# Middle group's rows dealt in turn, and four of 24 C products on GpSimd with their sums two units later

## Chip, cores and metric

The kernel runs on one core of a Trainium2 chip. The metric is the device time in microseconds of one execution. The kernel before takes 13000.71 us (median of 3 runs, 12998.91 to 13001.96).

## What is computed

Two metaformer layers over an input of 2 x 96 x 128 x 128 (float32). Layer 0 mixes tokens with four selective scans (Mamba): along the rows, along the rows backwards, along the columns and along the columns backwards. Layer 1 mixes them with a 3x3 convolution. Each mixer and each feed-forward network follows a layer norm and is added to its input. Nearly all of the time is in the scans:

```python
xz = x @ in_w.T;  xc, z = split(xz)              # 192 + 192 channels per direction
xc = silu(causal_conv4(xc) + conv_b)
dt_raw, Bm, Cm = split(xc @ xproj_w.T)           # 6, 16 and 16 values per token
dt = softplus(dt_raw @ dt_w.T + dt_b)
h = exp(dt * A) * h + dt * B_t * u_t             # per channel, 16 states, 16384 tokens in turn
y = sum over the 16 states of h * C_t
out = ((y + Dp * xc) * silu(z)) @ outp_w.T       # then the four directions are fused by fuse_w
```

## The kernel before

**Steps, groups, units.** Per image (two of them) the scan stage runs over two pairs of directions, (0, 2) and (1, 3), each in 32 tiles of T = 512 tokens: 64 steps per image, 128 in all. The two directions of a pair have 2 x 192 = 384 channels, which are 3 groups of 128 partitions. Group 1, the middle one, holds the last 64 channels of the first direction in partitions 0 to 63 and the first 64 of the second in partitions 64 to 127. A unit is one group and two of the 16 states, (g, s) in the code, so a step has 24 units: 0 to 7 are group 0, 8 to 15 group 1, 16 to 23 group 2.

**What a unit does.** GpSimd multiplies a row tile of B by dt*u (`b_part`, L324). ScalarE makes two decays exp(dt*A) into PSUM (`decay`, L330). VectorE runs two scans of 512 tokens (`scan`, L334), which overwrite the decays in PSUM, and one product with C over both states (L409), which overwrites the C rows in SBUF. ScalarE copies the last state to `hst` (L410). TensorE adds the two products to y in PSUM with an identity matrix (`sums`, L341). At a group's first unit y starts with Dp*xc (L416), after `gated` (L349) has taken the previous group's y; y has one PSUM buffer.

**Rows.** B and C are needed on all 128 partitions. `rows_out` (L255) copies the 96 rows of one step to SBUF and writes four copies to DRAM (`bcd`, L261). `row_tile` (L312) reads them back, broadcast over the partitions: 128 x 4 states x 512, 1 MB, for two units. A group 1 tile comes in two DMAs of 64 partitions. B has four such buffers, C has three (`bufs=ahead + 1`).

**The order is written by hand.** `in_order` keeps every engine in program order, SP's queue of DMA issues too; a DMA that must wait for its buffer holds all that stands behind it on SP. Iteration k of the main loop issues: on even k the fetch of B for units k+6 and k+7; GpSimd's product with B for unit k+2; the pieces listed for (k, 0); the first scan of unit k; `behind(k-1)`, which is the product with C, the state copy and the sums of unit k-1; the second scan; on even k the fetch of C for units k+4 and k+5; the decays of unit k+2; the pieces listed for (k, 1). `later` puts a piece into a later iteration.

**The next step's preparation** is spread over the 24 units by the list `at` (L301): loads at 0, the convolution of groups 0 to 2 on TensorE at 4, 5, 6 (`conv`, copied out by ScalarE in `conv_out`, L233), the gates at 7, 10, 11 (`gate`, `gate_out`, L241), silu of all of xc at (8, 1) and of sz at (14, 1) (L244, with an activation table load before and after), the rows at 12, and dt in three chains from 13, 18 and 21. All of these, `project` (L352, in iterations 3 and 19) included, use the one PSUM bank `misc`, so each waits until ScalarE has emptied the bank of the one before.

Of the kernel before, what the change touches and what calls it, by code (L numbers as in the profile page):

```python
# [10 lines left out]
F32 = mybir.dt.float32  # L11
# [3 lines left out]
AF = mybir.ActivationFunctionType  # L15
# [5 lines left out]
C = 96  # L21
W = 128
L = W * W
T = 512
# [4 lines left out]
DI = 192  # L29
HID = 384  # L30
PAIRS = ((0, 2), (1, 3))
NG = 3
# [1 line left out]
B_AHEAD = 3  # L34
C_AHEAD = 2
AHEAD = 2
BY_POOL = ()
BCO = 32
NBC = 4 * S

# [2 lines left out]
def tile_metaformer(ctx: ExitStack, tc: tile.TileContext, a: dict, out: bass.AP):  # L43
    nc = tc.nc
# [22 lines left out]
    convb = const("convb", (128, 2, NG))  # L67
    bcw = const("bcw", (128, 2, NG, BCO + NBC))
    dtw = const("dtw", (2 * RK, 2, NG * 128))
# [6 lines left out]
    dmat = cpool.tile([128, 2, NG, 128], F32, name="dmat")  # L76
    gmat = cpool.tile([128, 2, NG + 1, C], F32, name="gmat")
    inx = cpool.tile([C, 4, 4, DI], F32, name="inx")
    nc.vector.memset(gmat, 0.0)
    with tc.tile_pool(name="prep", bufs=1) as pp, tc.tile_pool(name="prep_ps", bufs=2, space=PSUM) as pps:  # L80
        alog = pp.tile([128, 2, NG, S], F32, name="alog")
        nc.sync.dma_start(alog, a["alog"])
        nc.scalar.activation(alog, alog, AF.Exp)
        nc.vector.tensor_scalar_mul(amat, alog, -1.0)

        dskip = pp.tile([128, 2, NG], F32, name="dskip")
        nc.sync.dma_start(dskip, a["dskip"])
        for pi in range(2):
            for g in range(NG):
                nc.vector.tensor_scalar_mul(dmat[:, pi, g, :], ident, dskip[:, pi, g : g + 1])  # L90

        inxw = pp.tile([C, 4, DI], F32, name="inxw")
        nc.sync.dma_start(inxw, a["inx"])
        taps = pp.tile([C, 4, 4, DI], F32, name="taps")
        nc.sync.dma_start(taps, a["taps"].broadcast_to((C, 4, 4, DI)))
        for d in range(4):
            nc.vector.tensor_tensor(inx[:, d], taps[:, d], inxw[:, d, None, :].broadcast_to((C, 4, DI)), ALU.mult)
        outw = pp.tile([C, 4, DI], F32, name="outw")
        nc.sync.dma_start(outw, a["outw"])
        fusew = pp.tile([C, 4, C], F32, name="fusew")  # L100
        nc.sync.dma_start(fusew, a["fusew"])
        for pi, (da, db) in enumerate(PAIRS):

            pieces = [
                (slice(0, 128), da, 0, 128),
                (slice(0, 64), da, 128, 192),
                (slice(64, 128), db, 0, 64),
                (slice(0, 128), db, 64, 192),
            ]
            for g, (rows, d, lo, hi) in enumerate(pieces):  # L110
                ps = pps.tile([128, C], F32, name="ps")
                nc.tensor.matmul(ps[rows, :], outw[:, d, lo:hi], fusew[:, d, :], start=True, stop=True)
                nc.vector.tensor_copy(gmat[rows, pi, g, :], ps[rows, :])

    def layernorm(x, eps, dst, wp, psp, bufs=2, **cast):

# [66 lines left out]
    def mamba(acc, xnr, xnc):  # L183

        with ExitStack() as st:
# [24 lines left out]
            def prologue(pi, i, d):  # L210
# [19 lines left out]
                def conv_out(g):  # L230
                    if g == 0:
                        d["xc"] = two.tile([128, NG, T], F32, name="xc")
                    nc.scalar.activation(d["xc"][:, g, :], d["ps"], AF.Identity, bias=convb[:, pi, g : g + 1])  # L233

                def gate(g):
                    d["ps"] = inproj(pi, g, lambda dd, k, lo, hi: inz[:, dd, lo:hi], src, (3,))
# [1 line left out]
                def gate_out(g):  # L238
                    if g == 0:
                        d["sz"] = two.tile([128, NG, T], F32, name="sz")  # L240
                    nc.scalar.copy(d["sz"][:, g, :], d["ps"])  # L241

                def silu(name):
                    nc.scalar.activation(d[name], d[name], AF.Silu)  # L244
# [8 lines left out]
                        )  # L253

                def rows_out():  # L255

                    d["rows"] = one.tile([BCO + NBC, T], F32, name="rows")
                    nc.scalar.copy(d["rows"], d["ps"][0 : BCO + NBC, :])
                    d["bcd"] = rows_d.tile([COPIES, 2, NBC // 2, T], F32, name="bcd")
                    for n in range(COPIES):  # L260
                        nc.sync.dma_start(d["bcd"][n].rearrange("k r t -> (k r) t"), d["rows"][BCO:, :])  # L261
# [37 lines left out]


                at = [(0, 0, load), (8, 1, partial(silu, "xc")), (14, 1, partial(silu, "sz"))]  # L301
                at += [(12, 0, rows), (12, 1, rows_out)]
                for g, k in enumerate((4, 5, 6)):
                    at += [(k, 0, partial(conv, g)), (k, 1, partial(conv_out, g))]
                for g, k in enumerate((7, 10, 11)):
# [6 lines left out]
            def row_tile(d, g, s, k, ahead):  # L312

                t = gen.tile([128, 4, T], F32, name=f"row{k}", bufs=ahead + 1)
                for half in range(2) if g == 1 else (slice(None),):
                    rows = slice(half * 64, half * 64 + 64) if g == 1 else half
                    at = s + S * (half if g == 1 else g // 2)
                    n = (64 if g == 1 else 128) // COPIES
                    src = d["bcd"][None, :, k, at : at + 4, :].broadcast_to((n, COPIES, 4, T))
                    nc.sync.dma_start(t[rows], src)  # L320
                return t
# [17 lines left out]
            def sums(s, y, c):  # L339
                for j in range(2):  # L340
                    nc.tensor.matmul(y, ident, c[:, j, :], start=False, stop=s + j == S - 1)  # L341

            def by_pool(s, y, h, c):
                nc.gpsimd.tensor_tensor(c, h, c, ALU.mult)
                sums(s, y, c)

            def gated(pi, d, g, y):
                t = d["sz"][:, g, :]
# [26 lines left out]
            def later(k, where, f, *args):  # L375
                todo.setdefault((k, where), []).append(partial(f, *args))
# [26 lines left out]
            def behind(k):  # L403

                n, u = divmod(k, nu)
                (pi, i), d, (g, s) = steps[n], state[n], units[u]
                h, c = hs.pop(k), cs.pop(k)
                if (g, s) not in BY_POOL:
                    nc.vector.tensor_tensor(c, h, c, ALU.mult)  # L409
                nc.scalar.copy(hst[:, g, s : s + 2], h[:, :, T - 1])  # L410
                if s == 0:
                    if k > 0:
                        pn, pu = divmod(k - 1, nu)
                        gated(steps[pn][0], state[pn], units[pu][0], ys.pop(k - 1))
                    y = ps_y.tile([128, T], F32, name="y")
                    nc.tensor.matmul(y, dmat[:, pi, g, :], d["xc"][:, g, :], start=True, stop=False)  # L416
                else:
                    y = ys.pop(k - 1)
                ys[k] = y
                if (g, s) in BY_POOL:  # L420
                    later(k + 1, 1, by_pool, s, y, h, c)
                else:
                    sums(s, y, c)
                if k == total - 1:
                    gated(pi, d, g, y)
                if s == S - 2 and g > 0:
                    later(k + 4, 0, project, pi, i, d, g)
                    later(k + 4, 1, collect, pi, d, g)
# [7 lines left out]
            for k in range(total + 6):  # L436
                n, u = divmod(k, nu)
                if u == 0 and n + 1 < len(steps):
                    for m, where, f in prologue(*steps[n + 1], state[n + 1]):
                        later(k + m, where, f)  # L440
                if k % 2 == 0:
                    fetch(k + 2 * B_AHEAD, 0, B_AHEAD, bs)
                feed(k + AHEAD)
                issue(k, 0)
                if k < total:
                    (_, i), (g, s) = steps[n], units[u]
                    da, b = das.pop(k), bs.pop(k)
                    hs[k] = b if (g, s) in BY_POOL else da
                    scan(i, g, s, 0, da, b, hs[k])
                if 0 < k <= total:  # L450
                    behind(k - 1)
                if k < total:
                    scan(i, g, s, 1, da, b, hs[k])
                if k % 2 == 0:
                    fetch(k + 2 * C_AHEAD, 1, C_AHEAD, cs)
                feed_decay(k + AHEAD)
                issue(k, 1)
# [108 lines left out]
def _layout(v):  # L566

    f = np.float32
    order = [d for pair in PAIRS for d in pair]
    rows = lambda w: w[order].reshape(2, NG, 128, -1).transpose(2, 0, 1, 3)  # L570
    xw = v["L0_conv_xproj_w"]
    bcw = np.zeros((2, 2 * DI, BCO + NBC), f)
    dtw = np.zeros((2 * RK, 2, 2 * DI), f)
    for pi, pair in enumerate(PAIRS):
        for k, d in enumerate(pair):
# [3 lines left out]
                bcw[pi, at, to] = xw[d, RK + j * S : RK + (j + 1) * S].T  # L579
            bcw[pi, at, k * RK : (k + 1) * RK] = xw[d, :RK].T  # L580
            dtw[k * RK : (k + 1) * RK, pi, at] = v["L0_conv_dt_w"][d].T
    grouped = lambda w: w.reshape(2, NG, 128, -1).transpose(2, 0, 1, 3)
    out = {
        "x": v["x"].reshape(NB, C, L),
        "ident": np.eye(128, dtype=f),
        "inx": v["L0_conv_in_w"][:, :DI].transpose(2, 0, 1),
        "inz": v["L0_conv_in_w"][:, DI:].transpose(2, 0, 1),
        "taps": v["L0_conv_conv_w"].transpose(0, 2, 1)[None],
        "convb": rows(v["L0_conv_conv_b"])[..., 0],
        "bcw": grouped(bcw),  # L590
        "dtw": dtw,
        "dtb": rows(v["L0_conv_dt_b"])[..., 0],
        "alog": rows(v["L0_conv_A_log"]),
        "dskip": rows(v["L0_conv_Dp"])[..., 0],
        "outw": v["L0_conv_outp_w"].transpose(1, 0, 2),
        "fusew": v["L0_conv_fuse_w"].reshape(C, 4, C).transpose(2, 1, 0),
        "fuseb": v["L0_conv_fuse_b"].reshape(C, 1),
        "kw": v["L1_conv_kernel"].transpose(1, 2, 3, 0).reshape(C, 9, C),
# [24 lines left out]
```

## Time and profile before

| | |
|---|---|
| median of 3 runs | 13000.71 us |
| profiled execution, own time | 13004.29 us |
| its span, first to last instruction | 13002.5 us |
| instructions | 97992 |
| DMA queue of SP, share of 16 engines | 83.1% |
| half row tiles (512 KB), issue to landing | 8.0 us, x2048 |
| whole row tiles (1024 KB), issue to landing | 7.5 us, x2048 |
| mean granted TensorE clock | 0.963 |

A group line of the page reads: source line, engine, operation, out<-in by the program's names, shapes, count, then busy us and mean ns of one, then the idle time of that engine just ahead of these instructions and what ended most of it. A TensorE product in float32 is two matmul instructions in the trace, so the sums of a unit are four. Engines overlap; [...] two instructions in a row start a little closer together than one lasts.

### The profile page before, as it was taken

To read this page: it belongs to the slowest core of one execution; us is meant where nothing else is said; L and a number is where in the kernel's file an instruction comes from. 1 tells how busy PE (TensorE), PEld (TensorE's weight loads), DVE (VectorE), ACT (ScalarE), POOL (GpSimd) and SP (SyncE) were. 2 spreads that over 40 slices of the span, in tenths; PEclk is the share of its full clock that TensorE was granted. 3 is DMA by queue.
4 is the path that set the end of the run, shared out by engine and by line. 5 is a ranking of instruction groups with operands and counts; after the bars stand their busy time and mean duration, and the time that the engine had idled before them with its cause. 6 is when DMAs were issued, how large, how long until landed. Compare 5 with 4: busy or idle time off the path is not lost. (4 is left out here: it accounts for less than half of the span.)

```text
span 13002.5 us, 97992 instructions
## 1 busy us (share of the span) xinstructions
PE 10850.3 (83%) x24208; PEld 3987.1 (31%) x24208; DVE 11569.1 (89%) x10865; ACT 8560.0 (66%) x14738; POOL 9215.4 (71%) x4772
## 2 busy tenths in 40 slices
PE   6888888888888888888978888888888888888889
PEld 2323233333333333333323333332333333333233
DVE  5999999999999999995459999999999999999954
ACT  6666666666666666665566666666666666666655
POOL 4877778777787787772147778777787777877721
PEclk8999999999999999999989999999999999999999
DMA  7999999999999999992079999999999999999920
GB/s 226 287 294 282 298 288 285 295 283 298 288 285 295 283 295 289 285 295 68 13 226 285 298 283 292 290 285 298 285 291 291 284 298 286 290 294 281 296 61 13
DMA packets 545331, 3400.40 MB, mean 262 GB/s; under 512 B 81612, under 2 KB 82732, under 8 KB 146840
## 3 DMA queue, kind: packets, MB, share of 16 engines
q1 hardware_dynamic: 544760, 3394.12, 83.1%
q8 instruction: 195, 3.19, 0.1%
q14 instruction: 376, 3.08, 0.1%
HBM read 3288.94 MB, written 104.86 MB: 261 GB/s over the span
## 5 line engine op out<-in xcount | busy, mean ns | idle before, releaser
L324 POOL TENSOR_TENSOR row<-dtu,row 128x1024 f32<-128x1024 f32 x3072 | 7175.7, 2358 | 1739.3 <-DMA row<-bcd 1419.2
L334 DVE TENSOR_TENSOR_SCAN da<-da,hst,row 128x512 f32<-128x512 f32 x5952 | 7339.4, 1274 | 351.2 <-ACT da L330 194.6
L341 PE MATMUL y<-row,ident 128*128 128x512 f32 x12288 | 6120.1, 626 | 1113.3 <-DVE row L409 1098.9
L330 ACT ACTIVATE da<-dt,amat 128x512 f32<-128x512 f32 x6144 | 4249.4, 692 | 207.5 <-ACT hst L410 0.4
L341 PEld LDWEIGHTS y<-row,ident 128*128 128x128 f32 x12288 | 2288.9, 197 | 4779.4 <-DVE row L409 2292.3
L409 DVE TENSOR_TENSOR row<-da,row 128x1024 f32<-128x1024 f32 x3072 | 3705.9, 1206 | 19.6 <-DMA row<-bcd 18.8
L410 ACT COPY hst<-da 128x2 f32<-128x2 f32 x3072 | 484.0, 158 | 2235.5 <-DVE row L409 2233.3
L416 PE MATMUL y<-xc,dmat 128*128 128x512 f32 x768 | 526.1, 773 | 779.1 <-DVE sz L349 779.1
L287 POOL TENSOR_TENSOR q<-e,q 128x512 f32<-128x512 f32 x384 | 488.0, 1271 | 821.8 <-ACT hst L410 709.1
L233 ACT ACTIVATE xc<-misc,convb 128x512 f32<-128x512 f32 x384 | 264.2, 688 | 1117.5 <-PE misc L207 1117.5
L207 PE MATMUL misc<-xa,inx 96*128 96x512 f32 (+1 forms) x2048 | 932.4, 597 | 59.0 <-DMA xa<-xnr 57.2
L207 PE MATMUL misc<-xb,inx 96*64 96x512 f32 (+1 forms) x2048 | 928.1, 595 | 1.6 <-ACT xc L233 1.6
L531 POOL TENSOR_TENSOR acc<-acc,y 96x512 f32<-96x512 f32 x128 | 147.6, 1153 | 987.0 <-DVE y L530 987.0
L541 PE MATMUL pc<-pad,kw 96*96 96x512 f32 x1152 | 566.7, 593 | 0.0
L207 PEld LDWEIGHTS misc<-xa,inx 96*128 96x128 f32 (+1 forms) x2048 | 323.6, 163 | 625.5 <-issue 493.4
L293 POOL TENSOR_TENSOR dt<-dt,ln 128x512 f32<-128x512 f32 x384 | 486.9, 1268 | 30.1
L297 POOL TENSOR_TENSOR dtu<-dt,xc 128x512 f32<-128x512 f32 x384 | 488.5, 1272 | 0.5
L290 POOL TENSOR_TENSOR ln<-ln,q 128x512 f32<-128x512 f32 x384 | 488.1, 1271 | 0.5
L359 PE MATMUL misc<-sz,gmat 128*96 128x512 f32 x1024 | 483.6, 594 | 0.0
L416 PEld LDWEIGHTS y<-xc,dmat 128*128 128x128 f32 x768 | 129.0, 211 | 1102.1 <-DVE sz L349 1099.1
L268 PE MATMUL misc<-rows,dtw 12*128 12x512 f32 x768 | 439.7, 652 | 18.5 <-ACT dt L275 17.2
L132 DVE TENSOR_TENSOR xq<-xm,rs 96x512 fp8e5<-96x512 f32 x128 | 87.9, 687 | 387.8 <-ACT rs L128 387.8
(75 smaller groups left out, 8403.8 us busy)
## 6 DMA issues: line engine op xcount, KB each, us to landing
row<-bcd SPq DMA_DIRECT2D x2048, 1024.0 KB, 7.5
row<-bcd SPq DMA_DIRECT2D x2048, 512.0 KB, 8.0
bcd<-rows SPq DMA_DIRECT2D x512, 128.0 KB, 9.8
xa<-xnr SPq DMA_DIRECT2D x124, 193.1 KB, 5.8
xb<-xnc SPq DMA_DIRECT2D x124, 193.1 KB, 5.5
acc<-in_x_dram SPq DMA_DIRECT2D x16, 768.0 KB, 17.8
xnr<-xn SPq DMA_DIRECT2D x16, 768.0 KB, 4.3
xnc<-stg SPq DMA_DIRECT2D x16, 768.0 KB, 5.6
```

The lines of the kernel that those rows point to most:

```text
L207: nc.tensor.matmul(ps[rows, :], w(PAIRS[pi][d], k, lo, hi), src[d][:, k : k + T], **se)
L287: nc.gpsimd.tensor_tensor(d["q"], d["e"], d["q"], ALU.subtract)
L290: nc.gpsimd.tensor_tensor(d["ln"], d["ln"], d["q"], ALU.add)
L293: nc.gpsimd.tensor_tensor(d["dt"][g], d["dt"][g], d["ln"], ALU.add)
L297: nc.gpsimd.tensor_tensor(dtu, d["dt"][g], d["xc"][:, g, :], ALU.mult)
L324: nc.gpsimd.tensor_tensor(b, d["dtu"][g][:, None, :].broadcast_to((128, 2, T)), b, ALU.mult)
L330: nc.scalar.activation(da[:, j, :], d["dt"][g], AF.Exp, scale=amat[:, pi, g, s + j : s + j + 1])
L334: nc.vector.tensor_tensor_scan(h[:, j, :], da[:, j, :], b[:, j, :], 0.0 if i == 0 else hst[:, g, s + j : s + j + 1], ALU.mult, ALU.add,)
L341: nc.tensor.matmul(y, ident, c[:, j, :], start=False, stop=s + j == S - 1)
L409: nc.vector.tensor_tensor(c, h, c, ALU.mult)
L416: nc.tensor.matmul(y, dmat[:, pi, g, :], d["xc"][:, g, :], start=True, stop=False)
L541: nc.tensor.matmul(pc, kw[:, t, :], rows, start=t == 0, stop=t == 8)
```

## The change

1. The rows of group 1 are dealt in turn: even partitions carry the first direction, odd ones the second. A tile of B or C rows still comes in two DMAs of 64 partitions, now every second one. The weights of that group are permuted on the way in, and the output projection gets weights with zeros in the other direction's rows (`outx`).
2. The matmuls of the convolution and the gate [...] write as before, into halves; ScalarE copies to a tile `mix`, and two DMAs of 64 partitions move it into every second partition of xc (in iteration 7) and sz (in iteration 12).
3. Writing `bcd` to DRAM is a piece of its own, at (14, 0) instead of (12, 1).
4. Units (0, 2), (0, 8), (1, 2) and (1, 8), which are units 1, 4, 9 and 12 of a step, scan into a tile `h` in SBUF (one buffer). Their product with C is GpSimd's, in the iteration after the scan, behind that iteration's product with B. Their sums are issued two iterations after those of other units would be.

```diff
-BY_POOL = ()
+BY_POOL = ((0, 2), (0, 8), (1, 2), (1, 8))
...
-        outw = pp.tile([C, 4, DI], F32, name="outw")
-        nc.sync.dma_start(outw, a["outw"])
+        outx = pp.tile([C, 2, NG + 1, 128], F32, name="outx")
+        nc.sync.dma_start(outx, a["outx"])
...
+            for g in range(NG + 1):
                 ps = pps.tile([128, C], F32, name="ps")
-                nc.tensor.matmul(ps[rows, :], outw[:, d, lo:hi], fusew[:, d, :], start=True, stop=True)
-                nc.vector.tensor_copy(gmat[rows, pi, g, :], ps[rows, :])
+                nc.tensor.matmul(ps, outx[:, pi, g, :], fusew[:, pair[g // 2], :], start=True, stop=True)
+                nc.vector.tensor_copy(gmat[:, pi, g, :], ps)
...
-                    nc.scalar.activation(d["xc"][:, g, :], d["ps"], AF.Identity, bias=convb[:, pi, g : g + 1])
+                    t = mixed("xc") if g == 1 else d["xc"][:, g, :]
+                    nc.scalar.activation(t, d["ps"], AF.Identity, bias=convb[:, pi, g : g + 1])
...
-                    nc.scalar.copy(d["sz"][:, g, :], d["ps"])
+                    nc.scalar.copy(mixed("sz") if g == 1 else d["sz"][:, g, :], d["ps"])
+
+                def mixed(name):
+                    d["mix", name] = one.tile([128, T], F32, name="mix")
+                    return d["mix", name]
+
+                def mix(name):
+
+                    for k in range(2):
+                        nc.sync.dma_start(d[name][k:128:2, 1, :], d["mix", name][64 * k : 64 * k + 64, :])
...
                     d["rows"] = one.tile([BCO + NBC, T], F32, name="rows")
                     nc.scalar.copy(d["rows"], d["ps"][0 : BCO + NBC, :])
+
+                def rows_to_dram():
+
                     d["bcd"] = rows_d.tile([COPIES, 2, NBC // 2, T], F32, name="bcd")
...
-                at += [(12, 0, rows), (12, 1, rows_out)]
+                at += [(12, 0, rows), (12, 1, rows_out), (14, 0, rows_to_dram)]
+                at += [(7, 0, partial(mix, "xc")), (12, 0, partial(mix, "sz"))]
...
-                    rows = slice(half * 64, half * 64 + 64) if g == 1 else half
+
+                    rows = slice(half, 128, 2) if g == 1 else half
...
-            def by_pool(s, y, h, c):
+            def by_pool(h, c):
                 nc.gpsimd.tensor_tensor(c, h, c, ALU.mult)
-                sums(s, y, c)
...
                 if (g, s) in BY_POOL:
-                    later(k + 1, 1, by_pool, s, y, h, c)
+                    later(k + 1, 1, by_pool, h, c)
+                    later(k + 3, 1, sums, s, y, c)
...
-                    hs[k] = b if (g, s) in BY_POOL else da
+                    hs[k] = one.tile([128, 2, T], F32, name="h") if (g, s) in BY_POOL else da
```

More of the change, by code (lines that the diff above doesn't have):

```diff
@@ L78, in tile_metaformer @@
     inx = cpool.tile([C, 4, 4, DI], F32, name="inx")
-    nc.vector.memset(gmat, 0.0)
     with tc.tile_pool(name="prep", bufs=1) as pp, tc.tile_pool(name="prep_ps", bufs=2, space=PSUM) as pps:
@@ L97, in tile_metaformer @@
             nc.vector.tensor_tensor(inx[:, d], taps[:, d], inxw[:, d, None, :].broadcast_to((C, 4, DI)), ALU.mult)
-        outw = pp.tile([C, 4, DI], F32, name="outw")
-        nc.sync.dma_start(outw, a["outw"])
+        outx = pp.tile([C, 2, NG + 1, 128], F32, name="outx")
+        nc.sync.dma_start(outx, a["outx"])
         fusew = pp.tile([C, 4, C], F32, name="fusew")
         nc.sync.dma_start(fusew, a["fusew"])
[L102 to L110, printed above, removed]
+        for pi, pair in enumerate(PAIRS):
+            for g in range(NG + 1):
                 ps = pps.tile([128, C], F32, name="ps")
-                nc.tensor.matmul(ps[rows, :], outw[:, d, lo:hi], fusew[:, d, :], start=True, stop=True)
-                nc.vector.tensor_copy(gmat[rows, pi, g, :], ps[rows, :])
+                nc.tensor.matmul(ps, outx[:, pi, g, :], fusew[:, pair[g // 2], :], start=True, stop=True)
+                nc.vector.tensor_copy(gmat[:, pi, g, :], ps)
     def layernorm(x, eps, dst, wp, psp, bufs=2, **cast):
@@ L569, in _layout @@
     order = [d for pair in PAIRS for d in pair]
-    rows = lambda w: w[order].reshape(2, NG, 128, -1).transpose(2, 0, 1, 3)
+    perm = np.arange(2 * DI)
+    perm[128:256] = perm[128:256].reshape(2, 64).T.reshape(-1)
+    grouped = lambda w: w.reshape(2, NG, 128, -1).transpose(2, 0, 1, 3)
+    plain = lambda w: grouped(w[order].reshape(2, 2 * DI, -1))
+    rows = lambda w: grouped(w[order].reshape(2, 2 * DI, -1)[:, perm])
     xw = v["L0_conv_xproj_w"]
@@ L581, in _layout @@
             dtw[k * RK : (k + 1) * RK, pi, at] = v["L0_conv_dt_w"][d].T
-    grouped = lambda w: w.reshape(2, NG, 128, -1).transpose(2, 0, 1, 3)
+    outx = np.zeros((C, 2, NG + 1, 128), f)
+    for pi, (p, q) in enumerate(PAIRS):
+        ow = v["L0_conv_outp_w"]
+        outx[:, pi, 0] = ow[p, :, :128]
+        outx[:, pi, 1, 0::2] = ow[p, :, 128:]
+        outx[:, pi, 2, 1::2] = ow[q, :, :64]
+        outx[:, pi, 3] = ow[q, :, 64:]
     out = {
@@ L588, in _layout @@
         "taps": v["L0_conv_conv_w"].transpose(0, 2, 1)[None],
-        "convb": rows(v["L0_conv_conv_b"])[..., 0],
-        "bcw": grouped(bcw),
-        "dtw": dtw,
+        "convb": plain(v["L0_conv_conv_b"])[..., 0],
+        "bcw": grouped(bcw[:, perm]),
+        "dtw": dtw[:, :, perm],
         "dtb": rows(v["L0_conv_dt_b"])[..., 0],
@@ L594, in _layout @@
         "dskip": rows(v["L0_conv_Dp"])[..., 0],
-        "outw": v["L0_conv_outp_w"].transpose(1, 0, 2),
+        "outx": outx,
         "fusew": v["L0_conv_fuse_w"].reshape(C, 4, C).transpose(2, 1, 0),
```

## The prediction

> **What bounds the kernel now.** I read the page's first part and its costliest groups first. (A measurement of this kernel tells about 0.2%, 26 us, from no change; "same" below means within that.)
>
> ```profile
> PE 10850.3 (83%) x24208; PEld 3987.1 (31%) x24208; DVE 11569.1 (89%) x10865; ACT 8560.0 (66%) x14738; POOL 9215.4 (71%) x4772
> L324 POOL TENSOR_TENSOR row<-dtu,row 128x1024 f32<-128x1024 f32 x3072 | 7175.7, 2358 | 1739.3 <-DMA row<-bcd 1419.2
> L334 DVE TENSOR_TENSOR_SCAN da<-da,hst,row 128x512 f32<-128x512 f32 x5952 | 7339.4, 1274 | 351.2 <-ACT da L330 194.6
> L409 DVE TENSOR_TENSOR row<-da,row 128x1024 f32<-128x1024 f32 x3072 | 3705.9, 1206 | 19.6 <-DMA row<-bcd 18.8
> ```
>
> VectorE looks like the bound: its scans and products with C alone are 11 of 13 ms. But a share is a mean over stages, so I took one step of the 128 (1967.41 to 2058.1, 90.7 us) and asked for the busy times of three stretches of it. Columns: length, then busy time of PE, PEld, DVE, ACT and POOL, granted clock, DMA share, GB/s.
>
> ```profile
> 1973.00:2005.50 32.50, 31.52 (x74) 12.27 (x74) 29.01 (x27) 16.81 (x31) 27.38 (x14) 0.95 0.83 215
> 2005.50:2033.00 27.50, 22.29 (x48) 7.56 (x48) 26.39 (x23) 22.67 (x36) 12.69 (x7) 1.00 1.02 293
> 2033.00:2063.70 30.70, 22.43 (x44) 8.11 (x44) 30.65 (x27) 21.30 (x40) 30.54 (x18) 0.94 0.93 361
> ```
>
> The first stretch, about units 1 to 9, belongs to TensorE: 31.52 of 32.50 us, while VectorE has 3.5 us idle. The second is VectorE's with a stall at its end; the third is VectorE's and GpSimd's together. The timelines of the engines show how TensorE holds the first stretch, and two queues matter later:
>
> ```profile
> 1995.83 3.60 PE L207 MATMUL misc<-xb,inx 96*128 96x512 f32 x8
> 1999.27 1.88 PE L341 MATMUL y<-row,ident 128*128 128x512 f32 x4
> 2001.18 0.52 SPq L320 DMA_DIRECT2D row<-bcd  x1
> 1999.47 0.69 ACT L233 ACTIVATE xc<-misc,convb 128x512 f32<-128x512 f32 x1 [3.16 <-PE misc L207]
> 2001.76 1.29 DVE L334 TENSOR_TENSOR_SCAN da<-da,hst,row 128x512 f32<-128x512 f32 x1 [1.75 <-ACT da L330]
> 2005.49 0.69 DVE L349 TENSOR_TENSOR sz<-y,sz 128x512 f32<-128x512 f32 x1 [1.33 <-PE y L341]
> 2004.16 1.28 ACT L244 ACT_TABLE_LOAD   x1
> 2005.46 1.48 ACT L244 ACTIVATE xc<-xc 128x1536 f32<-128x1536 f32 x1
> 2008.45 1.42 ACT L330 ACTIVATE da<-dt,amat 128x512 f32<-128x512 f32 x2
> ```
>
> The convolution of the next step ends on PE, ScalarE's copy of it waits 3.16 us, the decay queued behind that copy is late, and the scan waits 1.75 us. Then VectorE waits 1.33 us for the last sum of group 0. The SP line is the fetch of C for units 10 and 11: it leaves 0.03 us after the sums of unit 5 end (1999.27 + 1.88), since it takes over their buffer. The queue's own waits confirm that this is the rule:
>
> ```profile
> SPq L320 <- PE y L341: 4676.5, 1476, 8.1
> ```
>
> [...] So all that SP holds behind a waiting fetch is late too; the line above agrees. [...] 221 GB/s in 2010:2013 with halves in flight, 393 in 2024:2035. [...] I count no contention; the trace's 2358 ns for GpSimd beside a busy VectorE agrees. [...] The trace has PEclk 0.50 in 1975.19:1978.60, after 2.10 us of waiting, 3.41 us long.
>
> **The change, part by part.** Times are within the step (view less 1967.41). Pitches from the timelines: a unit is 3.49 us on VectorE (product 1.15, scans 2.34), four sums 1.73 on PE, a convolution group 3.44, the projection 2.6, a product on GpSimd 2.33.
>
> *Products removed.* Units 1, 4, 9, 12: 4 x 1.15 = 4.6 us a step. Those of units 1 and 4 fall in the TensorE stretch, which still holds every sum of group 0 between the gated products at 5.8 and 38.1. They gain nothing there. Units 9 and 12 could gain 2.3.
>
> *Their products on GpSimd.* 2.36 each by the nearest row (L324, same size), 9.4 a step. GpSimd feeds units 3 and 4 only 0.6 and 0.5 us ahead of their scans, and there is one states tile: unit 4's scan waits for unit 1's product, which runs 14.0 to 16.4 behind the feed of unit 4. The scan slips from 14.5 to 16.4, later ones less; TensorE does not need that product before 20, so this stays hidden. Scan into SBUF: not in the trace; I take 1.27 as now, at most 0.1 either way, 0.8 us a step.
>
> *TensorE.* From 6.5 it does the start of y, sums 0 and the projection at half clock and then sums 2 up to 16.6, convolution 0 to 20.0, sums 3 and the deferred sums 1 to 23.5, convolution 1 to 27.0. In between convolutions 1 and 2 sums 4 used to stand and hid ScalarE's emptying of the one misc bank; now 0.6 us of pipeline and 0.69 of copy are bare, and convolution 2 runs 28.3 to 31.8. Sums 5, gate 0, sums 6, the deferred sums 4: to 37.9. Sums 7: to 39.6, so the gated product is at 40.2 instead of 38.1. Unit 11 would start at 44.3 (40.2 + 0.6 gated + 1.2 scan + 2.3 for unit 10, with its product gone) instead of 43.4.
>
> *SP and the new moves.* Of the three C buffers the first to come free for units 10 and 11 is that of units 4 and 5, now with sums 4: signalled at 38.5, not 33.7. The moves of xc stand behind this fetch (iteration 7 behind 6). Two fetch halves at 0.6 us of issue, two moves at 0.6: the last leaves at 40.3. Alone in the queue, 1 MB lands in 5.1 us (the DMA view at 2043.5), of which 2.5 is transfer at 420 GB/s; so the fetch lands at 43.4, and the two moves, 128 KB each behind it on the same engines, about 43.8. ScalarE's silu, which ran at 38.05, waits until then. Behind it stand table load, state copy and the decay of unit 11: 4.4 us from the start of silu to the end of that pair in the trace (2005.46 to 2009.87). That decay is done at 48.2 and unit 11 starts at 48.2, 4.8 us later than before. What cover was there, 0.9 us, is included.
>
> *The same once more for sz.* C for units 14 and 15 now waits for sums 11 of iteration 12 (the sums of unit 9 stand even behind those). Unit 12 starts 51.6; gate 2, rows and sums 11 on PE end with a signal at 57.8. If PE's idle time, 44.6 to 50.3, costs one half-clock window (3.4 us, so 1.7 of work lost), at 59.5: I take this. Behind it on SP: two halves, B of units 18 and 19, two moves: landed 8.3 us later, 67.8. Silu of sz, table load 1.3, three parts of the softplus 2.0 and the decay of unit 17 follow, 6.4 us: unit 17 starts at 74.2, where it was 65.6. So +8.6 a step. After unit 17 both kernels run alike; C for units 18 and 19 waits for sums 12 but has 10 us to spare. The later bcd writes (iteration 14) are one unit later and have four to land.
>
> *Rows in turn.* Halves at twice the rate: their gain lies in feeds that VectorE doesn't wait for (GpSimd's 1419 us of DMA waits against 19.6 idle before L409), so nothing by itself; it is in the 2.5 us above. Preparation and constants: a few us once, nothing.
>
> Sum: 126 steps have a next step to prepare, 126 x 8.6 = 1084, less some 9 for the last two. The profiled execution took 13004.29 around a span of 13002.5, 4 us over the median 13000.71. On that median: 14,076, say 14,080.
>
> **Rivals.** (1) The sz wait is hidden because the bandwidth of the rows in turn clears the queue: then 4.8 less 1.15 for unit 12 less the 1.06 stall now before unit 17 gives +2.6, 13,330. For it: the second replay is longer and less sure than the first. (2) Rows in turn don't spread: [...] a fetch of two halves takes 4.7 us instead of 2.5, so each of the two waits is 2.2 longer; 8.6 + 4.4, less about 1 that overlaps, is +12, 14,500. [...] (3) The moves land early enough: then only the TensorE stretch is later by 0.9, which units 12's 1.15 pays back: 13,000, no change. It needs SP to reach the moves by 34, against the measured rule. (4) VectorE is the bound and the waits fit: one mechanism, that the buffer of a deferred unit is not what SP waits for, from the point on where silu of xc starts before 40. Then units 9 and 12 save 2.3 (12,710), and at the very best all four 4.6, 585 us: 12,420. For it: 89% busy; against: 31.52 of 32.50.
>
> **How the numbers follow.** Forecast 0.60, (1) 0.15, (2) 0.13, (3) 0.04, (4) 0.08. The range runs from (1) to just over (2), 13,330 to 14,560, leaving (3), (4) and tails out. Slower 0.88, same 0.03 (the centre of (3)), faster 0.09.
>
> **What would show it.** ScalarE's silu of xc with idle time released by the xc move, 4 to 7 us, in nearly every step; the same for sz at 3 to 5; VectorE's scans waiting for ACT da; SP's waits on PE y grown; the first stretch's PE still full. PE more often at half clock in the middle of the step. Wrong if silu doesn't wait, or if SP issues the fetch of C for units 10 and 11 before the sums of unit 4.

## The result: 15.3% slower, and the profile after

The changed kernel takes 14,990.86 us (median of 4 runs, 14,984.99 to 15,005.47) against 13,000.49 us before: a ratio of 1.1533, 95% interval 1.1513 to 1.1553. The loss is 1,990 us, or about 15.5 us in each of the 126 to 128 steps. The forecast was 14,080 (+8.6 us a step), in a range up to 14,560: right in direction, much too small. The profiled execution's span is 15,003.7 us, its mean granted TensorE clock 0.890 (0.963 before).

These are lines of the page after. As before, a group line gives busy us, mean ns, then idle time just ahead and its releaser.

```profile
PE 11380.8 (76%) x24208; PEld 4288.4 (29%) x24208; DVE 11105.5 (74%) x10352; ACT 8498.5 (57%) x14738; POOL 10387.4 (69%) x5284
L331 POOL TENSOR_TENSOR row<-dtu,row 128x1024 f32<-128x1024 f32 x3072 | 7182.4, 2352 | 1102.8 <-DMA row<-bcd 1037.8
L341 DVE TENSOR_TENSOR_SCAN da<-da,hst,row 128x512 f32<-128x512 f32 x4960 | 6183.6, 1277 | 1688.2 <-ACT da L337 990.2
L415 DVE TENSOR_TENSOR row<-da,row 128x1024 f32<-128x1024 f32 x2560 | 3092.3, 1208 | 695.5 <-DMA row<-bcd 686.7
L351 POOL TENSOR_TENSOR row<-h,row 128x1024 f32<-128x1024 f32 x512 | 1205.2, 2354 | 449.8 <-DVE h L341 447.8
L341 DVE TENSOR_TENSOR_SCAN h<-da,hst,row 128x512 f32<-128x512 f32 x992 | 1262.5, 1273 | 330.0 <-POOL row L351 279.8
L247 ACT ACT_TABLE_LOAD x256 | 328.4, 1283 | 1765.5 <-DMA xc<-mix 1245.9
```

No engine has more work than before, apart from the products that GpSimd took over (1,205 us) and TensorE's matmuls at a lower clock. VectorE is busy 464 us less, and waits. The last line is the main one: ScalarE stands 1,765.5 us ahead of its 256 silu table loads, 1,245.9 of them for the moves of xc. In the kernel before, the same loads waited 4.5 us in all:

```profile
L244 ACT ACT_TABLE_LOAD x256 | 328.4, 1283 | 4.5
```

One step of the timeline, which starts at 2287.07 in this view, shows both waits and their followers:

```profile
2325.56 1.18 SPq L244 DMA_DIRECT2D xc<-mix  x2
2325.99 0.69 DVE L355 TENSOR_TENSOR sz<-y,sz 128x512 f32<-128x512 f32 x1 [2.15 <-PE y L348]
2332.99 1.28 ACT L247 ACT_TABLE_LOAD   x1 [10.05 <-DMA xc<-mix]
2334.28 1.48 ACT L247 ACTIVATE xc<-xc 128x1536 f32<-128x1536 f32 x1
2337.13 1.42 ACT L337 ACTIVATE da<-dt,amat 128x512 f32<-128x512 f32 x2
2338.65 1.29 DVE L341 TENSOR_TENSOR_SCAN da<-da,hst,row 128x512 f32<-128x512 f32 x1 [8.27 <-ACT da L337]
2340.54 2.07 PE L200 MATMUL misc<-xb,inz 96*128 96x512 f32 x2 [9.95 <-ACT mix L235]
2351.86 1.19 SPq L244 DMA_DIRECT2D sz<-mix  x2
2357.05 1.23 DVE L415 TENSOR_TENSOR row<-da,row 128x1024 f32<-128x1024 f32 x1 [4.15 <-DMA row<-bcd]
2360.43 1.28 ACT L247 ACT_TABLE_LOAD   x1 [4.29 <-DMA sz<-mix]
2368.15 1.29 DVE L341 TENSOR_TENSOR_SCAN da<-da,hst,row 128x512 f32<-128x512 f32 x1 [5.20 <-ACT hst L416]
```

Read it as a relay. SP issues the moves of xc at step time 38.5. They land, ScalarE loads the table at 45.9, silu runs, the decay of unit 11 follows, and VectorE, which stood 8.27 us, starts unit 11 at 51.6. TensorE stood 9.95 us for the gate's bank, which ScalarE had not emptied. Then sz goes the same way (the product that waits 4.15 us for C rows is unit 14's, issued in iteration 15), and unit 17 starts at 81.1 (65.6 before). From there the step runs as before.

The stretches with group 1's fetch and the moves in flight show the rate (columns as in the prediction: length, five busy times, clock, DMA share, GB/s):

```profile
2325.00:2329.00 4.00, 3.21 (x9) 1.18 (x7) 3.01 (x3) 0.00 (x0) 2.02 (x1) 1.00 1.03 244
2329.00:2332.50 3.50, 1.59 (x6) 0.20 (x4) 1.35 (x2) 0.00 (x0) 3.50 (x3) 1.00 1.04 234
```

The 16 DMA engines are full and move 234 to 244 GB/s. That is hardly more than the 221 of the halves before, and far from the 420 that the prediction took for rows in turn.

### The profile page after: what moved, and what is told of

It is laid out like the page before. It is cut to its first block, busy times and chain, and to the rows that moved or that the text cites. A ratio compares the mean times of both kernels' runs of the same rounds, so it can differ in the third digit from the quotient of the medians.

```text
span 15003.7 us, 100148 instructions
## 1 busy us (share of the span) xinstructions
PE 11380.8 (76%) x24208; PEld 4288.4 (29%) x24208; DVE 11105.5 (74%) x10352; ACT 8498.5 (57%) x14738; POOL 10387.4 (69%) x5284
## 5 line engine op out<-in xcount | busy, mean ns | idle before, releaser
L341 DVE TENSOR_TENSOR_SCAN da<-da,hst,row 128x512 f32<-128x512 f32 x4960 | 6183.6, 1277 | 1688.2 <-ACT da L337 990.2
L348 PE MATMUL y<-row,ident 128*128 128x512 f32 x12288 | 6450.4, 664 | 938.8 <-DVE row L415 935.1
L348 PEld LDWEIGHTS y<-row,ident 128*128 128x128 f32 x12288 | 2525.9, 212 | 4698.0 <-issue 2885.1
L415 DVE TENSOR_TENSOR row<-da,row 128x1024 f32<-128x1024 f32 x2560 | 3092.3, 1208 | 695.5 <-DMA row<-bcd 686.7
L416 ACT COPY hst<-da 128x2 f32<-128x2 f32 x2560 | 401.0, 157 | 2188.5 <-DVE row L415 2181.9
L351 POOL TENSOR_TENSOR row<-h,row 128x1024 f32<-128x1024 f32 x512 | 1205.2, 2354 | 449.8 <-DVE h L341 447.8
L341 DVE TENSOR_TENSOR_SCAN h<-da,hst,row 128x512 f32<-128x512 f32 x992 | 1262.5, 1273 | 330.0 <-POOL row L351 279.8
L422 PE MATMUL y<-xc,dmat 128*128 128x512 f32 x768 | 602.5, 877 | 1119.6 <-DVE sz L355 1119.6
L200 PE MATMUL misc<-xb,inz 96*64 96x512 f32 (+1 forms) x512 | 404.3, 882 | 1233.8 <-ACT mix L235 1215.0
L247 ACT ACT_TABLE_LOAD x256 | 328.4, 1283 | 1765.5 <-DMA xc<-mix 1245.9
L278 ACT ACTIVATE e<-misc,dtb 128x512 f32<-128x512 f32 x384 | 262.7, 684 | 507.5 <-PE misc L273 477.7
```

The lines of the kernel that those rows point to most:

```text
L200: nc.tensor.matmul(ps[rows, :], w(PAIRS[pi][d], k, lo, hi), src[d][:, k : k + T], **se)
L341: nc.vector.tensor_tensor_scan(h[:, j, :], da[:, j, :], b[:, j, :], 0.0 if i == 0 else hst[:, g, s + j : s + j + 1], ALU.mult, ALU.add,)
```

## The experiments

Two theories stood at the start. *Queue*: the moves stand on SP behind a fetch that the deferred sums delay, and ScalarE pays. *Rate*: group 1's rows in turn are no faster than halves, so whatever stands behind them is later still. A rival to both: the products on GpSimd themselves cost the time. All times are medians; "before" ran beside each and stayed within 12,999 to 13,005.

**Rows and moves alone.** 13,681.58, ratio 1.0523 [1.0507, 1.0538].

```diff
-BY_POOL = ((0, 2), (0, 8), (1, 2), (1, 8))
+BY_POOL = ()
```

> The changed kernel with no unit on GpSimd: rows in turn, moves through the mix tile and the later bcd writes stay. Queue theory (the moves stand on SP behind fetches of C that wait for sums): the moves of xc still stand behind the fetch of C for units 10 and 11, which waits for sums 5 only (33.8 within the step, not 37.2), so silu of xc is late by some 4 to 5 us a step and silu of sz hardly: 13,500 to 13,700 us. Rival (the products on GpSimd and the deferred sums cost by themselves, the moves little): within 13,000 to 13,100.

A hit. In one step silu of xc waits 4.64 us for the moves, from its table load on, and unit 11 waits 3.72 us:

```profile
2112.76 1.28 ACT L247 ACT_TABLE_LOAD   x1 [4.64 <-DMA xc<-mix]
```

So 681 us come with no product on GpSimd at all. The run doesn't part queue and rate: the moves stand behind a fetch, and that fetch is in halves.

**Products alone.** 13,572.73, ratio 1.0443 [1.0425, 1.0460]. The kernel before, with this put in:

```diff
+BY_POOL = ((0, 2), (0, 8), (1, 2), (1, 8))
...
+                    later(k + 1, 1, by_pool, h, c)
+                    later(k + 3, 1, sums, s, y, c)
...
-                    hs[k] = b if (g, s) in BY_POOL else da
+                    hs[k] = one.tile([128, 2, T], F32, name="h") if (g, s) in BY_POOL else da
```

> The kernel before with the four units on GpSimd, states tile and deferred sums, but rows in halves and no moves. Queue theory: nothing urgent stands behind the late fetches; one wait of about 3 us for C in unit 15, the TensorE stretch later by 0.9, against up to 2.3 us saved and the 1.1 us stall at unit 17 hidden: 12,900 to 13,150 us. Rival: most of the loss is here, 14,000 or more.

A miss. The page's line for the product with C shows where the time goes:

```profile
L408 DVE TENSOR_TENSOR row<-da,row 128x1024 f32<-128x1024 f32 x2560 | 3089.3, 1207 | 979.6 <-DMA row<-bcd 961.4
```

VectorE waits 961 us for C rows (18.8 before). My reading, which this run alone doesn't prove: the deferred sums free the buffers of C late, SP then issues the held fetches in bursts, and a queue that runs a third of its bytes at about half rate (221 GB/s with halves in flight against 393 in 2024:2035, both in the kernel before) doesn't catch up. In one step the products of units 6, 8, 10 and 14, issued in iterations 7, 9, 11 and 15, wait 1.08, 2.11, 2.25 and 3.85 us; each is the first to use a newly fetched tile of C. The two parts, 681 and 573, make 1,254 of 1,990. The remaining 736 come only when both are there; that the moves then stand behind those late fetches fits the timeline above.

**Moves from ScalarE's queue.** 13,716.48, ratio 1.0548 [1.0533, 1.0564]. The moves leave right behind the copies, from another queue; all else is the changed kernel.

```diff
-                        nc.sync.dma_start(d[name][k:128:2, 1, :], d["mix", name][64 * k : 64 * k + 64, :])
+                        nc.scalar.dma_start(d[name][k:128:2, 1, :], d["mix", name][64 * k : 64 * k + 64, :])
...
-                at += [(7, 0, partial(mix, "xc")), (12, 0, partial(mix, "sz"))]
+                at += [(5, 1, partial(mix, "xc")), (10, 1, partial(mix, "sz"))]
```

> The changed kernel with the moves issued from ScalarE's own queue, right behind the copy that they read, so that no fetch stands before them. Queue theory: ScalarE's waits for the moves go, the waits for C in unit 15 stay: 13,000 to 13,400 us. Rival (products and deferral): 14,500 or more. A third reading (the moves are slow because the DMA engines are full, whoever issues them): ScalarE still waits for them, over 14,000.

The largest single repair, 1,274 us, and still short of what was expected. Silu of xc waits 4.50 us until 40.2, though its moves were issued at about 27.3: in between the DMA engines were full (a share of 1.02 or more, at 232 to 243 GB/s), whichever queue issued.

**Moves ahead of the fetch on SP.** 14,142.43, ratio 1.0877 [1.0861, 1.0893].

```diff
-                    if g == 0:
+                    if g == 1:
...
-                at += [(7, 0, partial(mix, "xc")), (12, 0, partial(mix, "sz"))]
+                at += [(6, 0, partial(mix, "xc")), (8, 0, partial(mix, "sz"))]
...
-                for g, k in enumerate((7, 10, 11)):
+                for g, k in enumerate((10, 7, 11)):
```

> The changed kernel with both moves put on SP ahead of the fetches that wait: xc in iteration 6 before the fetch of C for units 10 and 11, and, with the gate of group 1 computed first (7) and that of group 0 at 10, sz in iteration 8. Nothing else is changed. Queue theory: ScalarE's waits for the moves go, what is left is near the run with the products alone: 13,450 to 13,800 us. If the full DMA engines make the moves late by themselves, ScalarE still waits for them over 3 us a step: 14,000 or more.

848 us less, a miss all the same. Its timeline (this step starts at 2147.79):

```profile
2152.24 22.01 SPq L327 DMA_DIRECT2D row<-bcd  x10
2175.20 1.15 SPq L244 DMA_DIRECT2D xc<-mix  x2
2189.03 0.58 ACT L235 COPY mix<-misc 128x512 f32<-128x512 f32 x1 [7.88 <-DMA xc<-mix]
```

The moves leave at 27.4 and land near 41, behind the half tiles that the burst had put into the engines, which move 243 to 250 GB/s at a share of 1.01 or more meanwhile. ScalarE's copy of the gate waits for them, since `mix` has one buffer. So the place on SP was a part of the trouble, and the full engines another.

**One whole tile for group 1.** 14,540.61, ratio 1.1184 [1.1167, 1.1200]. Both halves of group 1 come in one DMA with the first direction's rows, so the second direction's half is not computed from its own rows.

```diff
-                for half in range(2) if g == 1 else (slice(None),):
+                for half in (slice(None),):
...
-                    n = (64 if g == 1 else 128) // COPIES
+                    n = 128 // COPIES
```

> The changed kernel with group 1 tiles fetched by one DMA over 128 partitions from the first direction's rows (the second direction's half of group 1 gets wrong rows). If dealing the rows in turn left the halves at about half the rate, each of the two waits gets 2 to 3 us shorter: 14,200 to 14,450 us, and the fetch of units 10 and 11 lands about 5 us after its issue, not 7.7. If the halves already ran at the full rate, only an issue of 0.6 us is saved twice: 14,800 to 14,950.

450 us less, a little short of the expected gain. The median packet of 8 KB takes 309 ns, where the slow ones of the changed kernel (450 to 700 ns) have a median of 558, and the fetch lands 5.8 us after its issue instead of 7.7.

**Both halves in one DMA, two ways.** Each direction's own rows, in one DMA of 128 partitions whose source is walked as 16 times 8 rows: 15,170.16, ratio 1.1667 [1.1650, 1.1685]. With the same DMA walked as 32 times 4 rows: 14,551.32, ratio 1.1190 [1.1173, 1.1206]. Between the two only this line differs:

```diff
-                    src = r[None, :, :, s : s + 4, :].broadcast_to((16, COPIES, 2, 4, T))
+                    src = r[None, 0:2, :, s : s + 4, :].broadcast_to((32, 2, 2, 4, T))
```

> The changed kernel with both halves of a group 1 tile in one DMA over 128 partitions, with the right rows in turn (copies and halves lie in one stride in DRAM, and bcd is written by two DMAs of 256 KB, not four of 128). If the half rate of 64-partition DMAs is what is lost, as in the run with whole tiles: 14,350 to 14,600 us, and 400 GB/s or more in the stretch of group 1. If it was the missing rows there that made that run faster: 14,900 or more.

> The changed kernel with one DMA for a group 1 tile as in the last such run, except that the source is walked as 32 times 4 rows (2 copies, 2 halves) and not 16 times 8. If the half rate comes with an outermost count of 16 in the DMA, whatever partitions it writes, this has the 420 GB/s of the other groups in the stretch of group 1 and the time of the run with whole tiles: 14,400 to 14,620 us. If it comes from reading two directions' rows: half rate again, 14,900 or more.

The first missed. The second hit in time; its rate, 355 GB/s while the moves go through, stays under the 420 expected. The pages' lines for the DMA queue (packets, MB, share of 16 engines' span), the 16 form first:

```profile
q1 hardware_dynamic: 565240, 3461.28, 74.1%
```

```profile
q1 hardware_dynamic: 565240, 3461.28, 62.1%
```

Same packets, same bytes. 74.1% of 15,165.5 us is 11,238, 62.1% of 14,553.6 is 9,038: 2,200 us of all 16 engines, or 2.1 us for each of the 1,024 tiles of group 1. So the walk of the source sets the rate here. It is not which partitions are written, since both forms write all 128 and both with the directions in turn. Three things change together in that line: the outermost count (16 or 32), the rows in one turn (8 or 4) and the copies that are read (four or two). The copies alone are not it: the whole tiles of the run above, 32 times 4 over all four copies, also take 62.1%. Count and rows in one turn are not parted, and why the one walk is slower stays open. The halves of both kernels, which are slow too, are walked as 16 times 4.

**Table load ahead of the wait.** 14,654.16, ratio 1.1273 [1.1255, 1.1292].

```diff
                 def silu(name):
+                    nc.scalar.preload_act_table_set("silu_and_others")
```

> The changed kernel with silu's activation table asked for in an instruction of its own just before silu, which reads nothing and so doesn't wait for the move. If the table load stands behind the wait in the changed kernel, two loads of 1.28 us a step leave the chain: 14,600 to 14,750 us. If it doesn't matter, within 0.2% of the changed kernel, 14,991.

A hit: 337 us, where two loads of 1,283 ns in 126 steps are 323. The table load of the silu waits with it; one issued by hand ahead does not, and the wait now stands before the silu itself:

```profile
L248 ACT ACTIVATE xc<-xc 128x1536 f32<-128x1536 f32 x128 | 189.8, 1483 | 1085.4 <-DMA xc<-mix 1085.4
```

**All three together.** Tile by one DMA of 32, moves ahead, table ahead, the four units as in the change: 13,194.67, ratio 1.0146 [1.0130, 1.0161].

> The changed kernel, its four units on GpSimd as they were, with three causes taken away together: group 1's tile by one DMA with outermost count 32, the moves ahead of the fetches, the silu table loaded ahead of the wait. Apart they took 440, 848 and 337 us. Theory A (the waits for the moves and the late fetches are the whole loss): 13,050 to 13,350, the silu waits under 1 us, and what is left is unit 4's wait for the one states tile and TensorE's stretch. Theory B (the deferred sums alone cost some 500 us whatever the rows and moves are, as with the products alone): 13,400 to 13,650.

The first theory, and it takes back 1,796 of 1,990 us. Lines of its page:

```profile
L342 DVE TENSOR_TENSOR_SCAN da<-da,hst,row 128x512 f32<-128x512 f32 x4960 | 6169.5, 1275 | 434.6 <-ACT hst L417 360.1
L416 DVE TENSOR_TENSOR row<-da,row 128x1024 f32<-128x1024 f32 x2560 | 3086.6, 1206 | 36.7 <-DMA row<-bcd 33.5
L342 DVE TENSOR_TENSOR_SCAN h<-da,hst,row 128x512 f32<-128x512 f32 x992 | 1262.0, 1272 | 320.4 <-POOL row L352 279.7
```

The waits for C rows are down from 687 to 34 us, those for the silu are gone from the list. With these three causes gone, the deferred sums no longer make VectorE wait for rows. They don't pay either: the next run, without any product on GpSimd, is 141 us faster. What is left are unit 4's wait for the one states tile, TensorE's stretch and a 2.87 us wait of unit 17.

**No products at all, rows mended.** 13,053.34, ratio 1.0038 [1.0025, 1.0051]: tile by one DMA of 32, moves ahead, `BY_POOL = ()`.

> That one DMA, both moves ahead of the waiting fetches, no unit on GpSimd. If the moves were late for the queue on SP and for the DMA engines busy at half rate, both are gone and nothing else of the rows in turn costs anything: 12,900 to 13,050 us. If the moves cost by themselves (ScalarE waits for them over 2 us a step): 13,250 or more.

Just above the expected span. Rows at the rate of the 32 form bring nothing when VectorE doesn't wait for them: the stalls that remain are at the same three places as before (1.50, 1.67 and 1.26 us at unit 9, the gated product and unit 17; before 1.75, 1.33 and 1.06).

**Do the products ever pay?** The next runs look for better places for them; "mended rows" are those of the last run. First, the kernel before with even units and the sums one iteration sooner, `((0, 4), (0, 8), (1, 4), (1, 8))`: 13,314.95, ratio 1.0242 [1.0227, 1.0258].

> The kernel with products on GpSimd alone (rows in halves, no moves), with other units: 2, 4, 10 and 12, the first of a pair each time, and their sums one iteration after those of other units, right behind the sums of the pair's second unit. If the loss of 573 us came from C buffers that are held two iterations longer, VectorE's waits for C rows in units 7, 9, 11 and 15 mostly go: 12,850 to 13,150 us. If it came from the products themselves (GpSimd's time, one states tile), it stays: 13,350 or more.

Between both. In one step the C waits are gone but one (2.37 us, the product of unit 14), yet units 2 and 4 follow so closely that unit 4's scan waits 5.28 us for the states tile, and group 0's last sums hold the gated product 3.04 us. Group 0 is TensorE's stretch, so I kept to group 1: units 10, 12 and 14, with `later(k + 2, 0, sums, s, y, c)`. On mended rows 14,310.40, ratio 1.1004 [1.0987, 1.1020]; on the rows of before 13,673.87, ratio 1.0515 [1.0498, 1.0533].

> As the last, with units 10, 12 and 14 on GpSimd and their sums at the start of the iteration two after the scan's, so that the C buffer is let go no later than by the pair's second unit. VectorE saves 3 x 1.15 us in the stretch that it binds: 12,550 to 12,850 us, the fastest of all. If GpSimd's products are a loss wherever they stand: 13,100 or more.

> The kernel before with those same three units on GpSimd and the same early sums, rows in halves, no moves. If the DMA engines, busy without a break through group 1 at half rate, set the time there, VectorE's gain turns into waits for C rows: 12,850 to 13,050 us. If not: 12,550 to 12,750.

Two bad misses with a cause in common; the timeline of the first:

```profile
2244.48 1.26 POOL L293 TENSOR_TENSOR q<-e,q 128x512 f32<-128x512 f32 x1 [10.31 <-ACT q L290]
2248.11 2.93 PE L348 MATMUL y<-row,ident 128*128 128x512 f32 x3 [9.46 <-POOL row L351]
```

Unit 14's product stands on GpSimd behind q, a piece of the softplus that waits 10.31 us for ScalarE. TensorE's sums wait 9.46 us for the product, and y with them. In the second TensorE waits 9.65 us at the same place. The test is to leave unit 14 out, `((1, 4), (1, 8))`: 12,910.76 on the rows of before, ratio 0.9929 [0.9917, 0.9942].

> The kernel before (its own rows, no moves) with units 10 and 12 alone on GpSimd, sums one iteration later, at its head. Theory A (with three units it was unit 14's product that lost: it stands on GpSimd behind q of group 0, which waits for the softplus chain): without unit 14 the two products save up to 2.3 us of VectorE a step, and what ScalarE's chain before unit 17 leaves of it counts: 0.8 to 2 us a step, 12,750 to 12,920. Theory B (a product on GpSimd loses wherever it stands, since its sums free the buffer of C late and the fetch on SP is late with it): 13,000 to 13,300.

A hit, and the fastest of all versions: 94 us under the kernel before. Its page, beside the 11,569 us of before:

```profile
PE 10800.9 (84%) x24208; PEld 4001.0 (31%) x24208; DVE 11328.0 (88%) x10609; ACT 8516.1 (66%) x14738; POOL 9808.9 (76%) x5028
L408 DVE TENSOR_TENSOR row<-da,row 128x1024 f32<-128x1024 f32 x2816 | 3398.4, 1207 | 193.8 <-DMA row<-bcd 187.9
```

VectorE has 241 us less to do and 94 are kept; its waits for C rows, 188 us where there were 18.8, are about as large as the rest. On mended rows the same two units lose, though: 13,660.03, ratio 1.0503 [1.0489, 1.0518]. So there unit 14 was only half of the loss, 650 of the 1,257 us between 14,310 and the 13,053 without products.

> The kernel with rows in turn by one DMA whose outermost count is 32, the moves ahead of the fetches, and units 10 and 12 alone on GpSimd, sums one iteration later. Theory A: from 13,053 without any product on GpSimd, 0.8 to 2 us a step less: 12,800 to 12,970; the fast rows leave more room for the late fetch of C than the rows of before. Theory B (GpSimd's products lose anywhere): 13,060 to 13,350.

Neither theory foresaw this much. One step of it:

```profile
2112.80 1.42 ACT L337 ACTIVATE da<-dt,amat 128x512 f32<-128x512 f32 x2 [2.65 <-DVE h L341]
2116.18 1.13 PE L200 MATMUL misc<-xb,inz 96*128 96x512 f32 x2 [2.56 <-ACT sz L235]
2118.10 5.43 PE L254 MATMUL misc<-xc,bcw 128*96 128x512 f32 x6 [0.79 <-ACT sz L235]
2139.54 1.29 DVE L341 TENSOR_TENSOR_SCAN da<-da,hst,row 128x512 f32<-128x512 f32 x1 [4.05 <-ACT hst L416]
```

The decay of unit 11 waits 2.65 us for the scan of unit 10 into h, which it doesn't on the rows of before; TensorE, held behind ScalarE, idles 2.56 us and then runs at half clock (0.50 in 2118:2124), so the six matmuls for the rows take 5.43 us (2.81 in the kernel that gains, at 1.00). dt is late, and unit 17 waits 4.05 us. Two suspects: that wait, or the changed order of the gates. The kernel that gains, with the gates as `(10, 7, 11)`: 12,937.08, ratio 0.9950 [0.9935, 0.9965]. This kernel, with the gates as `(7, 10, 11)` and the moves of sz at 11: 13,516.07, ratio 1.0396 [1.0379, 1.0413].

> The kernel before with units 10 and 12 on GpSimd (12,911), and only the order of the gates changed: group 1 in iteration 7, group 0 in 10, as the kernels with the moves ahead have it. Theory A (the 750 us that separate the kernel with fast rows from this one come from the decay of unit 11, which there waits 2.65 us for the scan of unit 10 into h; here it carries no such wait): 12,880 to 12,960. Theory B (they come from the order of the gates, which leaves TensorE without work behind the gate of group 0): 13,300 to 13,700.

> The kernel with fast rows and units 10 and 12 on GpSimd (13,660), with the gates in the order of before, so that the moves of sz stand in iteration 11; the moves of xc stay ahead. The decay of unit 11 carries its own wait for VectorE here too. Theory A (that wait is the cause): 13,400 to 13,800. Theory B (the gate order is): 12,850 to 13,100.

Both as the first theory says: the gates cost 26 us, and 144 with the moves of sz; the decay still waits 2.47 us in the second. So the order of the gates is not the main cause. That the wait of the decay is (it leads to the idle TensorE, the half clock and the late dt above) fits the timelines, but it was not removed by itself: argued, not shown. Why the kernels with the moves have it stays open.

## Why the prediction was wrong in size

**The step that failed** is "1 MB lands in 5.1 us, of which 2.5 is transfer at 420 GB/s; so the fetch lands at 43.4, and the two moves ... about 43.8", resting on "Halves at twice the rate". Measured: issue at 37.2, halves landed 42.4 and 44.9, the moves 45.9, at 234 to 244 GB/s. That is 2.1 us later than priced. From the fetch's issue to the landed moves 5.3 us were priced and 8.7 were measured; 1.3 of these 3.4 were hidden because the fetch left sooner than predicted, which was luck. The second replay took 10.5 us where 8.3 were priced, 2.1 or so again. The rate is about half of this excess: in the run with the 32 form the same two stretches took 7.0 and 9.2 us in one step, and that run gave back 440 us, 3.5 us a step. Why the moves land later than priced even then stays open; the price of 0.4 us for two moves behind a fetch was itself too low.

The full rate for halves over every second partition was my estimate: the whole tiles' 420 GB/s (410 to 437 in most slices of 2040:2052 of the kernel before), put in place of the 221 of its halves. No trace had shown that the partitions written set that difference. The 16 and 32 forms write all 128 partitions alike, move 227 to 229 and 355 GB/s in the stretches read, and differ by 2.1 us a tile. The 221 GB/s of before may have the same cause, since those halves are walked as 16 times 4 too; no run here parts the walk from the partitions for them.

**A second term was mis-sized.** "Behind it stand table load, state copy and the decay" was priced from the start of silu, with the load of the silu's own table taken as done. It stands behind the same wait. The load takes 1,283 ns in the traces of both kernels. Where it waits the kernel before could hardly show, since its silu loads waited 4.5 us in all; the experiment priced it, 337 us.

**The sum then closes.** Predicted 48.2 for unit 11, measured 51.6: 2.1 + 1.28 = 3.4. For unit 17, predicted 74.2, measured 81.1: 3.4 carried, 2.1 and 1.28 once more = 6.8. So 8.6 + 6.9 = 15.5 us a step, and 126 of them make 1,953 of the 1,990. The experiments say nearly the same: the 32 form gave back 440 us and the table load 337, together 777 of the 911 us by which the forecast was short. The two were not run together with nothing else.

**Point by point.**

- *TensorE's stretch*: gated product predicted at 40.2, measured 38.9 (38.1 before). Right in kind, 1.3 too late: between convolutions 1 and 2 TensorE stood 0.79 us, where an estimated 0.6 of pipeline and 0.69 of copy were priced; SP's fetch left 1.3 sooner for it, at 37.2 instead of 38.5.
- *One states tile*: unit 4's scan predicted at 16.4, measured 16.3, after 2.26 us of waiting. The wait stays with the others gone (280 us in the run with all three); what it costs was not tested.
- *GpSimd's product* 2.36 us and *scan into SBUF* 1.27 us: 2,354 ns (2,331 to 2,411 over all 512) and 1,273 ns, as priced.
- *The chain SP, move, silu, decay, scan*, twice a step: as told, with both waits (10.05 and 4.29 us, from the table load on; 4 to 7 and 3 to 5 were predicted).
- *C for units 14 and 15*: predicted to leave at 59.5, left at 62.9: the 3.4 of the first replay carried over. That VectorE's product of unit 14 would itself wait for it, 4.15 us, was not foreseen; the wait for sz ends later.
- *Rows in turn, "nothing by itself"*: shown with the 32 form, the moves ahead and no products: 13,053 against 13,000.
- *Units 9 and 12 could gain 2.3 us*: units 10 and 12, on the rows of before, gain 94 us in all, 0.7 us a step.
- *Rivals*: (2), rows in turn no faster than halves, had the half rate right, at 14,500. It took off 1 us for overlap that the sum above doesn't need, and shared the error on the table load. (1), (3) and (4) needed SP or the queue to be early, and neither was.

## What to carry to other kernels

Before a DMA is put between two instructions of a tight chain, count what stands ahead of it twice: on the issuing queue and in the DMA engines themselves; in the run from ScalarE's queue, another queue cured only the first, and silu of xc still waited 4.50 us. When an engine takes work over, ask what stands in front of that work on its own queue, and which buffer comes free later: on the rows of before, two products gained 0.7%, and a third one behind a waiting softplus turned that into a loss of 5%. And take a transfer's rate from a row of the trace with the same access pattern, not from the partitions it touches: the 16 and 32 forms touch the same 128, at 227 to 229 and 355 GB/s.

## What was not expected of the hardware

- A 1 MB broadcast read of 8 KB rows into 128 partitions ran at 227 to 229 GB/s when walked as 16 times 8 rows, and each tile took 2.1 us less of the engines when walked as 32 times 4, with the same bytes, packets and partitions.
- A table load placed for an activation waits with it: 10.05 us of idle time stand before the load, not before the silu.
- A gap of 2.56 us on TensorE was followed by matmuls at half clock (0.50 in 2118:2124), 5.43 us for six instead of 2.81. The 2.10 us of the kernel before had done the same (0.50 in 1975.19:1978.60); 0.79 us, in the kernel that gains, did not (1.00 in 2088:2094).
